# Other rates for the background work of VectorE in the first blocks of an RWKV and feed-forward layer, and three small transposes

## Chip, cores and metric

One core of one Trainium2 chip runs the whole layer. The metric is the device time of one execution in microseconds; of several executions the median counts. All data are 32-bit floats.

## What is computed

Input x has 2048 tokens of 512 channels. The reference, cut to what matters:

```python
def attn(x):                                  # x: tokens x 512
    h = layer_norm(x, ln1_g, ln1_b)
    hh = time_shift(h)                        # the token before, zero for the first
    k = (h * tm_mk + hh * (1 - tm_mk)) @ Wk.T
    v = (h * tm_mv + hh * (1 - tm_mv)) @ Wv.T
    r = (h * tm_mr + hh * (1 - tm_mr)) @ Wr.T
    x = x + sigmoid(r) * wkv(k, v, tm_first) @ Wo.T
    h = layer_norm(x, ln2_g, ln2_b)
    hh = time_shift(h)
    kk = (h * cm_mk + hh * (1 - cm_mk)) @ Wkey.T        # 2048 wide
    sr = sigmoid((h * cm_mr + hh * (1 - cm_mr)) @ Wcr.T)
    return x + sr * (silu(kk) @ Wval.T)

def ffn(h):
    gate, up = split(h @ w_gate_up.T, 2)                # 2 x 2048 wide
    return (silu(gate) * up) @ w_down.T

x = x + attn(layernorm(x))
x = x + ffn(layernorm(x))
```

Here wkv has an empty state: each token stands alone, so no recurrence runs along the tokens.

## The kernel before

**Blocks.** The tokens are cut into four blocks of 512. For each block b the kernel runs "units" on TensorE: k, r and v (time mix), out (Wo), gate (Wcr), four up units (Wkey), one down unit (Wval), and then for all blocks the feed-forward part. The order at the start is: k, r, v, out of block 0; k, r, v of block 1; gate of block 0; out of block 1; the up units and the down unit of block 0; then block 2 (lines 1335 to 1394).

**Products with fewer multiplications.** Most units (unit, line 541) multiply 2 x 2 blocks of matrices with seven products in place of eight. For that, sums of quarters of the weights are needed. prepare (line 147) makes them: GpSimd's queue loads the four raw quarters of a weight, VectorE makes four sums of 128 x 512, and GpSimd's queue stores each to memory. When a product needs a sum, weight (line 171) loads it over SyncE's queue into a ring of 12 buffers. The first units are plain (PLAIN, line 37; plain_unit, line 636): they use raw quarters and eight products. One product of eight records takes TensorE 1.73 us.

**Normalisation.** time_norm (line 757) treats one block: four moment steps on VectorE (bn_stats, bn_aggr), then affine (two small operations, var), then for block 1 the power -0.5 on GpSimd (line 413), four steps that scale 128 x 512 each into h (scaled, line 428), two pauses, then the transposes of h on TensorE, one chunk of four per step (transposed, line 440), with ScalarE taking each chunk out into hT. channel_norm (line 987) does the same for the second normalisation, and mix (line 488) blends hT with its shifted copy into the operand of a unit, with one blend on VectorE per chunk ("mix<-hT,vec,mix") and, for units that are not plain, four sums of the operand. residual (line 739) makes four steps of one small VectorE operation (shift) and one ScalarE operation.

first_block (line 824) handles block 0 without the planner. Its normed(j) makes moments, affine and the power on GpSimd (tile "two", line 842) for half of the block, and scales two 128 x 512 pieces into h. mixed(j) transposes them, and ScalarE and VectorE make the first operand of k. Ahead of that, TensorE runs 24 transposes of the identity matrix into the tile "warm" (lines 343 to 345) and 16 small products into accv and accx.

**The planner.** TensorE, VectorE and ScalarE run in the order in which the program writes instructions (manual_schedule, line 1331). Work beside the units stands in queues of generators: background (norms, mixes, residuals) and preps (the weight sums). After each product a unit calls tick (line 297), which decides how many background steps are written before the next product. Every VectorE operation adds its estimated time to spent (cost, line 208: 0.683 for a tensor operation over 512 elements, 0.535 for a scaling, 0.17 at least). The heart of tick is

```python
slack[0] = max(min(slack[0] + share[0] * length - spent[0], 2.5), -2.5)
credit[0] = min(credit[0] + credit[1], 2.0)
while slack[0] > 0 and (hot or background or preps):
    if preps and not hot and credit[0] >= 1 and prep_one():
        credit[0] -= 1
```

and otherwise one background step, with its cost taken off slack. So share is the part of TensorE's time that VectorE's background work may fill, and credit[1] is the number of weight sums per tick at most. A step that returns a value ("yield 1") is a pause: nothing more of that item in this turn, though another item may step; if none does, the tick ends. need (line 322) writes out whatever is left of an item when a unit requires it, and sets a positive slack to zero. need_sums (line 283) does so for weight sums. Operations put off with later (line 211) are written one or two products later and charged then.

share starts at SHARE0 = 0.95 and becomes SHARE = 0.88 after the first up unit of block 0 (line 1372). credit[1] is 0.7 from the first block's k unit on (line 1338), 0.67 after the first up unit of block 0 (line 1374), and 0.55 after the first up unit of block 1 (line 1376). Between two products the planner counts STEP = 1.72 us.

Of the kernel before, what the change touches and what calls it, by code (L numbers as in the profile page):

```python
# [9 lines left out]
F32 = mybir.dt.float32  # L10
# [5 lines left out]
P = 128  # L16
# [4 lines left out]
HB = TB // 2  # L21
# [1 line left out]
WAIT = 5  # L23
STEP = 1.72
SHARE = 0.88
SHARE0 = 0.95
WARM = 24
PP0 = -1e38

# [33 lines left out]
def rwkv_ffn_kernel(  # L63
# [9 lines left out]
    nc = tc.nc  # L73
# [11 lines left out]
    ps = ctx.enter_context(tc.tile_pool(name="ps", bufs=6, space=bass.MemoryType.PSUM))  # L85
# [16 lines left out]
    def tok_tile(name):  # L102
        return tokp.tile([P, NT, H], F32, tag="tok", name=name)

    def bank():
        return ps.tile([P, 2, HB], F32, tag="ps", name="ps")
# [82 lines left out]
    def load_x(b, queues=None):  # L189
        t = tok_tile("x")  # L190
        for k in range(NT):
            eng = queues[k] if queues else nc.sync
            paced(eng.dma_start(t[:, k, :], x_t[b][:, k, :]))
        return t
# [7 lines left out]
    slack = [0.0]  # L202
    share = [SHARE0]
    put_off = deque()
# [46 lines left out]
    credit = [0.0, 0.0]  # L251
# [64 lines left out]
    def push(name, gen, ready=None):  # L316
        background.append([ready, gen, name, False, background])
# [18 lines left out]
    ident = const.tile([P, P], F32, name="ident")  # L336
    make_identity(nc, ident)

    warm = const.tile([P, 1], F32, name="warm")
    nc.vector.memset(warm, 0.0)  # L340
    nc.scalar.activation(warm, warm, AF.Exp)

    pt = ps.tile([P, 2, HB], F32, tag="ps", name="warm")
    for _ in range(WARM):
        nc.tensor.transpose(pt[:, 0, 0:P], ident, ident)

# [17 lines left out]
    def constants():  # L364
        nc.vector.tensor_scalar(onem, vec[:, MK : CR + 1, :], -1.0, 1.0, ALU.mult, ALU.add)
        nc.vector.tensor_scalar(nfirst, vec[:, FIRST, :], -1.0, PP0, ALU.mult, ALU.add)
# [9 lines left out]
    def vcol(row, c):  # L376
        return vec[:, row, c : c + 1]
# [14 lines left out]
    def ts(out, *args):  # L392
        nc.vector.tensor_scalar(out, *args)  # L393
        cost(size(out), 0.1, 0.00085)

    def stt(out, *args):
        nc.vector.scalar_tensor_tensor(out, *args)  # L397
        cost(size(out))

    def moments(src, mv):  # L400
        for t in range(src.shape[1]):
            st = small.tile([P, 6], F32, tag="st", name="st")
            nc.vector.bn_stats(st, src[:, t, :])
            nc.vector.bn_aggr(mv[:, t, :], st)
            cost(512)
            cost(0)
            yield
# [71 lines left out]
    def op_tile(name):  # L479
        assert op_free(), name  # L480
        live_ops[0] += 1
        m = opp.tile([P, 7, 2, HB], F32, tag="op", name=name)
        return m, {"sums": set(), **{k: m[:, k] for k in range(7)}}
# [255 lines left out]
    def residual(b, xb, cols):  # L739

        x1 = tok_tile("x1")
        x1s[b] = x1
        for t, (mean, scale) in enumerate(cols):
            shift = small.tile([P, 1], F32, tag="shift", name="shift")
            stt(shift, mean, -1.0, scale, ALU.mult, ALU.mult)
            nc.scalar.activation(x1[:, t, :], xb[:, t, :], AF.Identity, bias=shift, scale=scale)
            spent[0] += 0.4
            yield

    def affine(var, mv):  # L750


        n = mv.shape[1]
        ts(var[:, :n], mv[:, :, 1], EPS, None, ALU.add)
        ts(var[:, n : 2 * n], mv[:, :, 1], 1.0 + EPS, EPS * EPS, ALU.mult, ALU.add)
# [68 lines left out]
    def first_block():  # L824


        xb = xin.pop(0)
        hT = htp.tile([P, NC, TB + 1], F32, tag="hT", name="hT_a")
        hTs[0, "a"] = hT
        h = tok_tile("h")  # L830
        m, B = op_tile("mix")
        ops[0, "k"] = B
        finished.add((0, "k"))
        cols = []

        def normed(j):
            mv = small.tile([P, 2, 2], F32, tag="mv", name="mv")
            yield from moments(xb[:, 2 * j : 2 * j + 2, :], mv)
            var = small.tile([P, 4], F32, tag="var2", name="var2")
            affine(var, mv)  # L840
            two = small.tile([P, 4], F32, tag="two", name="two")
            nc.gpsimd.tensor_tensor(two, var, mhalf[:, :4], ALU.pow)
            yield
            for t in range(2):
                cols.append((mv[:, t, 0:1], two[:, t : t + 1]))
                ts(
                    h[:, 2 * j + t, :],
                    xb[:, 2 * j + t, :],
                    mv[:, t, 0:1],
                    two[:, 2 + t : 3 + t],  # L850
                    ALU.subtract,
                    ALU.mult,
                )
                yield

        def mixed(j, other):
            at = slice(j * HB, (j + 1) * HB)
            by_one = slice(j * HB + 1, (j + 1) * HB + 1)
            for c in range(NC):
                pt = bank()  # L860
                for t in range(2):
                    nc.tensor.transpose(
                        pt[:, 0, t * P : (t + 1) * P],
                        h[:, 2 * j + t, c * P : (c + 1) * P],
                        ident,
                    )
                nc.scalar.activation(
                    hT[:, c, by_one],
                    pt[:, 0, :],
                    AF.Identity,  # L870
                    bias=vcol(LN1B, c),
                    scale=vcol(LN1G, c),
                )
                d = m[:, 2 * (c // 2) + j, c % 2, :]
                nc.scalar.activation(d, hT[:, c, at], AF.Copy, scale=onem[:, 0, c : c + 1])
                stt(d, hT[:, c, by_one], vcol(MK, c), d, ALU.mult, ALU.add)
                next(other, None)

        one, two = normed(0), normed(1)
        for _ in range(3):  # L880
            next(one)
        next(two)
        for _ in one:
            pass
        constants()
        nc.vector.tensor_copy(hT[:, :, 0:1], carry["a"])
        next(two)
        next(two)
        mixed(0, two)
        for _ in two:  # L890
            pass

        def second():
            mixed(1, iter(()))
            tails[0] = residual(0, xb, cols)
            nc.vector.tensor_copy(carry["a"], hT[:, :, TB : TB + 1])
            finished.add("norm0")
            slack[0] = spent[0] = 0.0

        return second  # L900
# [9 lines left out]
    def time_mix(b, name):  # L910
        row, n = {"k": (MK, WK), "r": (MR, WR), "v": (MV, WV)}[name]
        yield from mix((b, name), hTs[b, "a"], row, (b, n) in PLAIN)

    def push_mix(b, name, gen):
        norm = f"normb{b}" if name in ("cr", "ck") else f"norm{b}"

        alone = (0, "r") if (b, name) == (0, "v") else norm
        push((b, name, "t"), gen, lambda: {norm, alone} <= finished and op_free())
# [131 lines left out]
    def load_resid(b):  # L1050
        r = tok_tile("resid")
        paced(nc.sync.dma_start(r, resid[b]))
        loads[b] = r, load_x(b)
# [281 lines left out]
    second_half = first_block()  # L1335
    for n in "rv":
        push_mix(0, n, time_mix(0, n))
    credit[1] = 0.7
    k_unit(0)
    prepare_all(early, False, 2)  # L1340
    prepare_all([WVAL + 3] + [WK] + late, True, 1)
# [15 lines left out]
    for b in range(NB):  # L1357
        nxt = b + 2 < NB
        if nxt:
            xin[b + 2] = load_x(b + 2)  # L1360
        if b == NB - 1:
            load_resid(0)
        gate_unit(b)
        if b + 1 < NB:
            out_unit(b + 1)
        need((b, "ck"))
        if nxt:
            push(f"norm{b + 2}", time_norm(b + 2))
        for g in range(4):
            up_unit(b, g)  # L1370
            if b == 0:
                share[0] = SHARE
                if g == 0:
                    credit[1] = 0.67
            if b == 1 and g == 0:
                credit[1] = 0.55
            if g == 0:
                if nxt:
                    push_mix(b + 2, "k", time_mix(b + 2, "k"))
                    push_residual(b + 2)  # L1380
                    push_mix(b + 2, "r", time_mix(b + 2, "r"))
                if b + 1 < NB:
                    push(f"normb{b + 1}", channel_norm(b + 1))
                if nxt:
                    push_mix(b + 2, "v", time_mix(b + 2, "v"))
                if b + 1 < NB:
                    push_mix(b + 1, "cr", channel_mix(b + 1, "cr"))
                    push_mix(b + 1, "ck", channel_mix(b + 1, "ck"))
        if b == NB - 1:
            push((0, "z", "t"), ffn_in(0), op_free)  # L1390
        down_unit(b)
        if nxt:
            for n, u in (("k", k_unit), ("r", r_unit), ("v", v_unit)):
                u(b + 2)
# [95 lines left out]
```

## Time and profile before

| | us |
|---|---|
| three runs | 1239.83, 1241.60, 1241.62 |
| median | 1241.6 |
| the profiled execution, its own time | 1239.16 |
| its span from the first to the last instruction | 1237.4 |

| engine | busy us | share of the span | instructions |
|---|---|---|---|
| TensorE matmul | 1226.9 | 99% | 6516 |
| TensorE weight load | 1100.8 | 89% | 6516 |
| VectorE | 715.9 | 58% | 1321 |
| ScalarE | 359.4 | 29% | 666 |
| GpSimd | 155.1 | 13% | 278 |

In the profile PE is TensorE, PEld its weight load, DVE VectorE, ACT ScalarE, POOL GpSimd, SP SyncE; a q behind the name (SPq, POOLq) stands for its queue of DMA issues. L389 is line 389, out<-in names the tiles. A timeline row gives the start and the duration in microseconds, what ran and how often, and in brackets how long the engine had been idle before it and what it waited for. A row of the table of waits gives the total, the number and the longest of the waits of one kind.

VectorE's load is uneven. In a count by 40 slices of 31 us it is busy for 80% and more of the second to fourth slice (31 to 124 us) and of the sixth, while its mean is 58%.

### The profile page before, as it was taken

What the parts mean: (1) busy time and instruction counts of PE and PEld (TensorE: products, weight loads), DVE (VectorE), ACT (ScalarE), POOL (GpSimd) and SP (SyncE); (2) the same over time, 40 slices, a digit from 0 to 9 for tenths busy, and PEclk for the clock granted to TensorE, in tenths of its full rate; (3) what the DMA queues carried; (4) which work ended last, traced back from release to release, by engine and by line L of the source; (5) the groups of instructions that cost most, each with busy time, mean ns of one, the idle gap of its engine ahead of it and who ended that gap; (6) DMA issues with size and microseconds to landing.
All of it is one profiled execution on the core that took longest, in us unless ns stands there. A gap on an engine that the chain in (4) does not pass through costs nothing.

```text
span 1237.4 us, 18097 instructions
## 1 busy us (share of the span) xinstructions
PE 1226.9 (99%) x6516; PEld 1100.8 (89%) x6516; DVE 715.9 (58%) x1321; ACT 359.4 (29%) x666; POOL 155.1 (13%) x278
## 2 busy tenths in 40 slices
PE   9999999999999999999999999999999999999998
PEld 8888888888888888888888888998899888998898
DVE  5888587677675757532432365556546365462466
ACT  5534242242523425212311222212221222112211
POOL 2332322222212122221000000000000000000000
PEclk9999999999999999999999999999999999999999
DMA  5789997798887887897546655895469745785576
GB/s 195 257 273 300 312 346 265 251 335 296 286 258 244 294 273 241 257 322 261 153 142 193 216 144 156 267 338 152 145 186 306 270 142 152 244 292 160 151 215 213
DMA packets 140303, 294.06 MB, mean 238 GB/s; under 512 B 17576, under 2 KB 18744, under 8 KB 138936
## 3 DMA queue, kind: packets, MB, share of 16 engines
q1 hardware_dynamic: 117168, 219.99, 57.1%
q0 software_dynamic: 21440, 70.27, 15.9%
q10 hardware_dynamic: 1608, 2.65, 0.6%
q8 instruction: 53, 0.87, 0.3%
q14 instruction: 34, 0.28, 0.1%
HBM read 250.89 MB, written 41.95 MB: 237 GB/s over the span
## 4 chain that ended last, share of the span: by engine, by line
PE 93%; DMA 2%; DVE 1%; issue 1%; POOL 1%; ACT 1%; SPq 0%; DVEq 0%; ACTq 0%; POOLq 0%
PE ps L560 53%; PE ps L1214 14%; PE accv L560 10%; PE accx L560 10%; PE ps L662 4%; PE ps L445 1%; DMA w<-sum 1%; DMA raw<-in_w 1%; DMA row<-stats 1%; POOL q L152 0%; DMA x<-in_x 0%; DVE h L393 0%; ACT mix L498 0%; DVE resid L389 0%; DVE r L389 0%
## 5 line engine op out<-in xcount | busy, mean ns | idle before, releaser
L560 PE MATMUL ps<-zT,w 128*128 128x256 f32 x1280 | 289.5, 379 | 0.0
L560 PEld LDWEIGHTS ps<-zT,w 128*128 128x128 f32 x1280 | 241.9, 190 | 32.2
L560 PE MATMUL ps<-mix,w 128*128 128x256 f32 x960 | 220.0, 379 | 0.9 <-ACT u L591 0.9
L560 PEld LDWEIGHTS ps<-mix,w 128*128 128x128 f32 x960 | 181.9, 190 | 26.2 <-ACT u L591 1.7
L389 DVE TENSOR_TENSOR u<-u,accx 128x512 f32<-128x512 f32 x67 | 46.0, 686 | 137.1 <-ACT accx L595 137.1
L1214 PE MATMUL ps<-w,hid 128*128 128x128 f32 x832 | 104.5, 275 | 0.0
L560 PE MATMUL ps<-w,t 128*128 128x256 f32 x456 | 102.0, 379 | 0.0
L1214 PEld LDWEIGHTS ps<-w,hid 128*128 128x128 f32 x832 | 99.8, 192 | 0.8
L560 PEld LDWEIGHTS ps<-w,t 128*128 128x128 f32 x456 | 86.6, 190 | 11.7
L580 ACT COPY accv<-ps 128x512 f32<-128x512 f32 x67 | 38.2, 570 | 180.4 <-PE ps L560 177.6
L1214 PE MATMUL ps<-w,quads 128*128 128x128 f32 x704 | 89.0, 275 | 0.4 <-ACT r L1226 0.4
L1214 PEld LDWEIGHTS ps<-w,quads 128*128 128x128 f32 x704 | 84.2, 192 | 0.9 <-ACT r L1226 0.5
L595 ACT COPY accx<-ps 128x512 f32<-128x512 f32 x67 | 38.2, 571 | 159.5 <-PE ps L560 159.4
L389 DVE TENSOR_TENSOR u<-ps,u 128x512 f32<-128x512 f32 x67 | 46.3, 691 | 63.3 <-PE ps L560 63.2
L1308 POOL DMA_DIRECT2D out<-resid x12 | 8.6, 718 | 535.0 <-DVE resid L389 535.0
L591 ACT COPY u<-ps 128x512 f32<-128x512 f32 x67 | 39.2, 585 | 120.8 <-PE ps L560 120.8
L1226 ACT COPY r<-ps 128x128 f32<-128x128 f32 x112 | 29.8, 266 | 142.1 <-PE ps L1214 142.1
L389 DVE TENSOR_TENSOR raw<-raw 128x512 f32<-128x512 f32 x84 | 57.8, 688 | 12.3 <-issue 5.0
L560 PE MATMUL accv<-zT,w 128*128 128x256 f32 x256 | 60.6, 379 | 0.0
L560 PE MATMUL accx<-zT,w 128*128 128x256 f32 x256 | 60.5, 379 | 0.0
L560 PE MATMUL ps<-w,s 128*128 128x256 f32 x256 | 58.2, 379 | 0.0
L662 PE MATMUL ps<-mix,w 128*128 128x256 f32 x256 | 56.8, 380 | 1.1 <-DVE mix L397 1.1
(168 smaller groups left out, 1664.0 us busy)
## 6 DMA issues: line engine op xcount, KB each, us to landing
w<-sum SPq DMA_DIRECT2D x316, 256.0 KB, 3.4
w<-in_w SPq DMA_DIRECT2D x253, 256.0 KB, 3.4
w<-dd SPq DMA_DIRECT2D x112, 256.0 KB, 3.6
w<-d SPq DMA_DIRECT2D x48, 256.0 KB, 3.3
q<-in_w POOLq DMA_DIRECT2D x44, 256.0 KB, 6.2
sum<-q POOLq DMA_DIRECT2D x44, 256.0 KB, 4.6
raw<-in_w POOLq DMA_DIRECT2D x40, 256.0 KB, 5.8
sum<-raw POOLq DMA_DIRECT2D x40, 256.0 KB, 4.1
```

The costliest lines, as they stand in the source:

```text
L389: nc.vector.tensor_tensor(out, a, b, op)
L445: nc.tensor.transpose(flat[:, t * P : (t + 1) * P], h[:, t, c * P : (c + 1) * P], ident)
L560: mm = nc.tensor.matmul(pz[:, m, :], lhsT=lhsT, rhs=rhs, start=first and g == 0 and m == 0 and k == 0, stop=g == last and k == 1, skip_gro ...
L580: "z", A11, B11, True, pop_held, read=lambda: nc.scalar.copy(accv, acc["z"])
L591: nc.scalar.copy(tmp["u2"], acc["z"])
L595: nc.scalar.copy(accx, acc["z"])
L662: mm = nc.tensor.matmul(acc[i, j][:, m, :], lhsT=act[:, k, lo] if by_token else wg[:, k, lo], rhs=wg[:, k, :] if by_token else act[:, k, : ...
L1214: mm = nc.tensor.matmul(dst, lhsT=x[k][:, g, :], rhs=wt[:, g, :], start=first and g == 0, stop=g == 3, skip_group_check=True,)
L1226: nc.scalar.copy(st["r"][:, m, n * P : (n + 1) * P], st["z"])
L1308: eng.dma_start(out_t[b][:, tokens, cols], rs[b][:, tokens, cols])
```

## The change

It sets share to 1.0 from the start, until the last up unit of block 0 is written (it was 0.95, until the first up unit). It sets credit[1] to 0.64 up to the first up unit of block 0 (it was 0.7), and to 0.75 from there to the first up unit of block 1 (it was 0.67). In first_block it adds, after the power of the first half, three transposes of that power's result ("two", 128 x 4) into the tile "warm", which nothing reads.

```diff
-SHARE0 = 0.95
+SHARE0 = 1.0
...
-    pt = ps.tile([P, 2, HB], F32, tag="ps", name="warm")
+    pt = wt = ps.tile([P, 2, HB], F32, tag="ps", name="warm")
...
             nc.gpsimd.tensor_tensor(two, var, mhalf[:, :4], ALU.pow)
+            if j == 0:
+
+                for _ in range(3):
+                    nc.tensor.transpose(wt[:4, 0, 0:P], two, ident)
             yield
...
-    credit[1] = 0.7
+    credit[1] = 0.64
     k_unit(0)
...
             up_unit(b, g)
-            if b == 0:
+            if b == 0 and g == 0:
+                credit[1] = 0.75
+            if b == 0 and g == 3:
                 share[0] = SHARE
-                if g == 0:
-                    credit[1] = 0.67
             if b == 1 and g == 0:
                 credit[1] = 0.55
```

## The prediction

> **What bounds the kernel now.** I read the page first: its busy row, then the table of waits of TensorE, then the timelines of TensorE, VectorE, GpSimd and SyncE around each of those waits.
>
> ```profile
> span 1237.4 us, 18097 instructions
> PE 1226.9 (99%) x6516; PEld 1100.8 (89%) x6516; DVE 715.9 (58%) x1321; ACT 359.4 (29%) x666; POOL 155.1 (13%) x278
> ```
>
> TensorE sets the end. The change leaves its products as they are, so time can only come from its idle places or go into new ones. The table of its waits:
>
> ```profile
> PE ps L560 <- issue: 2.1, 1, 2.1
> PE warm L345 <- POOL ident masks.py:199: 1.4, 1, 1.4
> PE ps L662 <- DVE mix L397: 1.1, 1, 1.1
> PE ps L560 <- ACT u L591: 0.9, 2, 0.7
> PE ps L445 <- DVE h L393: 0.7, 1, 0.7
> ```
>
> Between the first product and the tail there are 2.1 + 0.9 + 0.7 = 3.7 us. That is the most the retuned rates can win, 0.3% of the time. The 2.1 us stand at 105 us, where the gate unit of block 0 starts (columns: start, duration, what; idle before in brackets):
>
> ```profile
> 105.03 0.69 DVE L389 TENSOR_TENSOR u<-ps,u 128x512 f32<-128x512 f32 x1 [0.38 <-PE ps L560]
> 105.64 0.68 DVE L389 TENSOR_TENSOR q<-q 128x512 f32<-128x512 f32 x1
> 106.24 2.73 DVE L397 SCALAR_TENSOR_TENSOR mix<-hT_b,vec,mix 128x512 f32<-128x512 f32 x4
> 107.08 2.18 PE L560 MATMUL ps<-w,mix 128*128 128x256 f32 x8 [2.09 <-issue]
> ```
>
> The label says "issue", but the order tells the cause. The four blends of the "cr" mix are put into VectorE's queue only when need((0, "cr")) forces them, behind the last addition of r_unit(1) and a weight sum (q<-q). The first blend ends near 106.95 and TensorE starts at 107.08.
>
> The 0.7 us stand at 44.6 us, where the transposes of block 1's h wait for VectorE:
>
> ```profile
> 38.31 0.24 DVE L393 TENSOR_SCALAR var<-mv 128x4 f32<-128x4 f32 x2
> 40.84 1.00 DVE L393 TENSOR_SCALAR h<-x,mv,two 128x512 f32<-128x512 f32 x2 [0.23 <-POOL two L413]
> 44.02 0.54 DVE L393 TENSOR_SCALAR h<-x,mv,two 128x512 f32<-128x512 f32 x1
> 43.28 0.60 PE L445 MATMUL ps<-ident,h 128*128 128x128 f32 x3
> 44.62 0.77 PE L445 MATMUL ps<-ident,h 128*128 128x128 f32 x5 [0.73 <-DVE h L393]
> ```
>
> VectorE has var at 38.55, GpSimd's root takes until 40.81, the fourth h starts at 44.02, and the transpose that reads it at 44.62.
>
> **Part 1, share 1.0 and credit 0.64 up to the first up unit.** Both are inputs of tick (lines 297 to 314): slack grows by share x 1.72 per tick, less what is charged, and while it is positive one step is put out, first a weight sum if credit is at least 1. So an exact order follows from the code. The charges are 0.683 for a 512-wide tensor op or sum, 0.853 for a moment step, 0.535 for an h, 0.57 for a residual step (0.17 + 0.4), 0.34 for affine, 0.17 + 0.4 for the first transposed chunk. r_unit(0) has eight ticks, r1 to r8. Slack starts at 0 (need resets it), and put-off additions charge 0.683 before r1, r2, r3, r5, r7. Four moment steps fill r1 to r3 in both kernels. From there, with slack after the tick:
>
> ```
>       before (0.95, 0.7)               after (1.0, 0.64)
> r3    -0.56                            -0.30
> r4    affine, 2 residual   -0.40       same                   -0.06
> r5    sum                  -0.14       sum, sum               -0.39
> r6    sum, h0, h1          -0.25       h0, h1, h2             -0.27
> r7    sum, h2              -0.52       sum, h3                -0.46
> r8    sum, h3              -0.11       2 residual, chunk 0    -0.45
> ```
>
> In r8 the new credit is 0.92 (0.64 after r6, 1.28 - 1 after r7, + 0.64), so no sum takes the slack of -0.46 + 1.72 = 1.26, and 1.26 - 0.57 - 0.57 still leaves 0.12 (time_norm's two pauses of lines 775 and 776 are each passed with a residual step in the same tick): chunk 0 of the transposes goes out at the end of r_unit(0). Before, chunk 0 came two ticks later, at 43.28. TensorE is in program order, so v_unit(0)'s products now stand behind those four transposes, and the whole TensorE queue behind them.
>
> When are they fed? The r unit ends at 17.04 + 104 x 0.2187 = 39.8 us (120 records run from 17.04 to 43.28; 104 of them are k and r). The work of VectorE up to var is the same, and it has no idle place from 27.1 us on, so the root still ends at 40.81. Then h0, h1, h2 at 0.46 each (40.84, 41.30, 41.76), the put-off e at 42.22, a sum at 42.82 (0.60 each by their starts), h3 at 43.42, and the fourth transpose 0.60 later by the row of before, at 44.02. TensorE has done 39.8 + 3 x 0.11 = 40.1 us of work by then: 3.9 us idle instead of 0.73, **a loss of 3.2 us**. Bounds: h0 to h3 back to back end at 42.7, a loss of 1.9; another 0.6 us op ahead, 3.8.
>
> For the gate unit I carry the same ledger on. Per tick the planner has 0.086 more to give out, and sums take 0.06 x 0.683 = 0.04 less. Over the 35 ticks up to there that is 4.4 us of its own time. channel_norm(0) gets its first moments 5 ticks earlier (before at 83.35), its transposes come 4 ticks earlier in one tick, and the first two blends of "cr" are put out 5 ticks ahead of the gate unit, the last two 3 ahead. One would do, so the wait goes: **a gain of 2.1 us**; at least 0.6, if only the one sum leaves the way. Four chunks of transposes in one tick need h3 of channel_norm(0), put out three ticks (5.2 us) before: by my chain of VectorE (moments, 1.4 us of root, four h) some 2.3 us early, no new wait. VectorE keeps up at share 1.0: an op charged 0.683 takes 0.60, so 1.72 charged is 1.51 us of a 1.73 us tick.
>
> **Part 2, credit 0.75 and share 1.0 through the up units.** From 107 us to the tail TensorE's only waits are the 0.65 and 0.22 us on ScalarE's u copy, behind a row load which the ledger leaves in its tick, so nothing is won. What is at risk is a sum that comes late. Sums of the four key units fall up to 4 ticks behind, with 7 or 8 ticks left to the load, and the ledger is level again at the last value group. The tight place is SyncE's queue:
>
> ```profile
> SPq L168 <- DMA sum<-raw: 13.4, 2, 9.2
> 179.50 13.37 SPq L168 DMA_DIRECT2D w<-sum  x4
> ```
>
> The fourth of these loads waits 9.2 us for the third sum of the last value group and holds all loads behind it until 192.9. It lands 3.4 us later; TensorE reads it at 198.46 + 3 x 1.73 = 203.6, so 7.3 us are in hand. In the new ledger that sum is one tick (1.7 us) later. Cost 0; without that cover it would be 1.7. Later sums come earlier, to nobody's gain.
>
> **Part 3, three root transposes.** They sit on TensorE ahead of the transposes of block 0's first h, which lead ScalarE, VectorE and the first product with no slack:
>
> ```profile
> 1.37 5.38 PE L345 MATMUL warm<-ident 128*128 128x128 f32 x24 [1.37 <-POOL ident masks.py:199]
> 7.89 1.06 PE L351 MATMUL accx<-ident 128*128 128x128 f32 x8
> 8.78 1.04 PE L862 MATMUL ps<-ident,h 128*128 128x128 f32 x8
> 6.41 1.04 POOL L842 TENSOR_TENSOR two<-var,mhalf 128x4 f32<-128x4 f32 x1 [5.10 <-DVE var L393]
> ```
>
> The root is there at 7.45, TensorE comes at 8.78, h is there: no wait, but 3 x 0.11 to 0.13 us: **+0.35 us**. Bounds: 0.2 with a shorter weight load, 0.65 at the slow rate of the first row (5.38 / 24 = 0.22).
>
> **Sum.** 0.35 + 3.2 - 2.1 = +1.45 us on the profiled execution: span 1237.4, with 1.76 around it 1239.16, so 1240.6. That execution lies 2.4 us under the median of the runs (1241.6; lowest 1239.83). I put the difference on the median: **1243.0**; own range +0 to +3.8, so 1241.6 to 1245.4.
>
> **Rivals.** (a) TensorE's rate falls after the long idle place: the likeliest slower case. The first row above is at 0.22 us per transpose, the third at 0.13 or less, though the granted clock reads 1.00 in both, so the trace has a slow state (transposes per half microsecond go from 4 to 7 at 7.5 us). Against: after 2.09 us of idle the product at 107.08 took 2.18 instead of 1.89, of which some 0.3 is its second blend, and no slow rate followed. For: no idle place of before is as long as 4.2 us with four transposes in it. If it decides, half the rate for at most as long as at the start (1.4 to 7.4) costs up to 3.0: 1243.0 to 1246.0, say 1245.3.
>
> [...]
>
> (b) The transposes of block 1 don't wait longer, because VectorE reaches var earlier than I think; the gate wait goes. Then -2.1 - 0.7 + 0.35 = -2.5: 1239.1. For: VectorE has 0.99 us idle at 26; against: the order of charges up to var doesn't change, and GpSimd's 2.17 us root lies between. (c) A sum comes over 7.3 us late, SyncE's queue runs dry: +1.45 + 3 = 1246; against it the single tick of delay. (d) That the change does nothing to the order would leave +0.35; the ledger excludes it.
>
> **Numbers.** Forecast 59%, (a) 28%, (b) 9%, (c) 4%. 0.2% (2.5 us) is about what a measurement can tell from no change. Faster: 7 of (b)'s 9. Slower: (a) but for 1, (c), and 12 of the forecast's upper end: 43. The rest, 50, lies within. The range runs from 1240.2 (a forecast that falls on a low run, as the profile did) to 1246.1 (the end of (a)).
>
> **What would show it.** L445 with some 4 us before it near 40 to 44 us, and v_unit(0)'s first product after it (step 1); no wait at the gate unit (part 1's gain); L662's first product near 11.2 instead of 10.88 (part 3); products at twice 0.22 us a record after 44 us would be (a). I am wrong if the first chunk of block 1 is not ahead of v_unit(0).

## The result, and the profile after

| | before | after |
|---|---|---|
| runs side by side on one chip | 11 | 11 |
| median us | 1240.86 | 1244.06 |
| lowest and highest | 1238.88, 1241.62 | 1243.19, 1244.88 |
| ratio of the times, with its 95% interval | | 1.0027 (1.0018 to 1.0037) |
| profiled execution: time, span | 1239.16, 1237.4 | 1244.06, 1242.0 |

The changed kernel is slower by some 3.3 us (0.0027 x 1240.86; 2.2 to 4.6 by the interval). The forecast was 1243.0, which is 1.45 us above the median of the three runs of before, and the range held the time. The case forecast, with no change of the clock, wasn't what happened: rival (a), the slower rate of TensorE after its long wait, came on top of it, and so did waits that the prediction had put at nothing. The profiled execution of before lies 1.7 us under the median of its eleven runs and that of the changed kernel on its median, so the two traces differ by more (4.9 us in time, 4.6 in span) than the medians do (3.2). The page of the changed kernel:

```profile
span 1242.0 us, 18100 instructions
PE 1229.2 (99%) x6519; PEld 1101.8 (89%) x6519; DVE 714.8 (58%) x1321; ACT 358.9 (29%) x666; POOL 154.7 (12%) x278
```

There are three more TensorE instructions (the root transposes), as many VectorE and ScalarE instructions as before, and a span that is 4.6 us longer. TensorE is busy 2.3 us longer, which three small transposes can't account for: the same products took longer. The table of TensorE's waits:

```profile
PE ps L445 <- DVE h L393: 3.1, 2, 1.8
PE ps L560 <- ACT u L591: 1.4, 2, 1.1
PE warm L345 <- POOL ident masks.py:199: 1.4, 1, 1.4
PE ps L560 <- ACT accx L595: 1.1, 2, 0.9
PE ps L662 <- DVE mix L397: 1.1, 1, 1.1
PE ps L1218 <- ACT r L1230: 0.4, 1, 0.4
```

The "issue" line of 2.1 us is gone. The wait for h has grown from 0.7 to 3.1 us in two parts, the waits for ScalarE's copies u from 0.9 to 1.4, and a line for its copies accx is new. No wait for a load of a weight appears. The timeline of TensorE around these places:

```profile
37.79 1.89 PE L662 MATMUL ps<-mix,w 128*128 128x256 f32 x8
41.47 1.24 PE L445 MATMUL ps<-ident,h 128*128 128x128 f32 x3 [1.79 <-DVE h L393]
44.04 0.33 PE L445 MATMUL ps<-ident,h 128*128 128x128 f32 x1 [1.33 <-DVE h L393]
44.21 5.31 PE L662 MATMUL ps<-mix,w 128*128 128x256 f32 x16
49.35 1.47 PE L445 MATMUL ps<-ident,h 128*128 128x128 f32 x12
...
109.93 1.89 PE L560 MATMUL ps<-w,mix 128*128 128x256 f32 x8
...
165.40 1.89 PE L560 MATMUL accx<-mix,w 128*128 128x256 f32 x8
168.38 5.45 PE L560 MATMUL ps<-mix,w 128*128 128x256 f32 x24 [1.09 <-ACT u L591]
174.72 1.99 PE L560 MATMUL ps<-mix,w 128*128 128x256 f32 x8 [0.89 <-ACT accx L595]
```

The four transposes of the first chunk stand ahead of v_unit(0), as the ledger gave it; behind them come two of its products (16 records), then the other twelve transposes. The row of 1.24 us for three transposes has idle time in it that the brackets don't show, since each waits for its own h: a transpose takes some 0.11 (the twelve at 49.35 start 0.11 apart). The fourth starts at 44.04. The gate unit starts at 109.93 with no wait. The row at 44.21 is the one to look at: 16 records in 5.31 us, while another row of 16 records (106.47, of the r unit) takes 3.62. The table by stretches of 1 us shows why (columns: stretch, its length, TensorE's busy time and records, granted clock, share of the DMA engines, GB/s):

```profile
43.00:44.00 1.00, 0.00 (x0) 1.00 0.65 246
44.00:45.00 1.00, 0.96 (x4) 0.71 0.09 37
45.00:46.00 1.00, 1.00 (x4) 0.50 0.60 225
46.00:47.00 1.00, 1.00 (x4) 0.50 0.32 98
47.00:48.00 1.00, 1.00 (x4) 0.59 0.43 164
48.00:49.00 1.00, 1.00 (x7) 1.00 0.04 8
```

Four records per microsecond while the granted clock is 0.50, seven just after it: the starts of the products' records lie 0.43 us apart before 47.8 us and 0.22 apart from there on. The half rate lasts 0.58 + 1 + 1 + 0.82 = 3.4 us (0.71 over a microsecond is 0.58 of it at half rate, 0.59 is 0.82), so it costs 1.7 us. VectorE's timeline of the same place:

```profile
38.34 0.24 DVE L393 TENSOR_SCALAR var<-mv 128x4 f32<-128x4 f32 x2
...
39.23 1.41 DVE L389 TENSOR_TENSOR q<-q 128x512 f32<-128x512 f32 x2
40.87 1.46 DVE L393 TENSOR_SCALAR h<-x,mv,two 128x512 f32<-128x512 f32 x3 [0.23 <-POOL two L413]
42.25 0.68 DVE L397 SCALAR_TENSOR_TENSOR e<-sg,e 128x512 f32<-128x512 f32 x1
42.85 0.68 DVE L389 TENSOR_TENSOR q<-q 128x512 f32<-128x512 f32 x1
43.45 0.54 DVE L393 TENSOR_SCALAR h<-x,mv,two 128x512 f32<-128x512 f32 x1
```

The prediction had these starts at 40.84, 42.22, 42.82 and 43.42 and the fourth transpose at 44.02; all came within 0.03 us. Between var and the h lies GpSimd's root, which took 2.17 us in both traces.

Where the span's 4.6 us come from, by comparing the start of each TensorE record with its predecessor's in both traces:

| place | forecast us | measured us |
|---|---|---|
| start, up to the first product | +0.35 | 0 |
| r unit of block 0 no longer waits for its mix (28.5 us) | 0 | -0.2 |
| transposes of block 1's h | +3.2 | +3.3 (4.2 idle, less 0.95) |
| half clock behind them | 0 (rival (a)) | +1.7 |
| gate unit of block 0 | -2.1 | -2.25 |
| a copy accx in a unit of block 1's time mix (99 us) | 0 | +0.4 |
| copies u and accx in the up and down units (167 to 341 us) | 0 | +1.9 |
| sum | +1.45 | +4.8 |

The sum is 0.2 over the measured difference, which is what such reading of single records leaves.

### The profile page after: what moved, and what is told of

It is laid out like the page before. It is cut to its first block, busy times and chain, and to the rows that moved or that the text cites. A ratio compares the mean times of both kernels' runs of the same rounds, so it can differ in the third digit from the quotient of the medians.

```text
span 1242.0 us, 18100 instructions
## 1 busy us (share of the span) xinstructions
PE 1229.2 (99%) x6519; PEld 1101.8 (89%) x6519; DVE 714.8 (58%) x1321; ACT 358.9 (29%) x666; POOL 154.7 (12%) x278
## 4 chain that ended last, share of the span: by engine, by line
PE 93%; DMA 2%; DVE 2%; issue 1%; ACT 1%; POOL 1%; SPq 0%; DVEq 0%; POOLq 0%; ACTq 0%
PE ps L560 52%; PE ps L1218 14%; PE accv L560 11%; PE accx L560 10%; PE ps L662 5%; PE ps L445 1%; DMA row<-stats 1%; DMA w<-sum 1%; DMA raw<-in_w 1%; DVE xT L389 1%; PE warm L345 0%; POOL q L152 0%; DVE t L389 0%; DVE q L389 0%; DVE resid L389 0%
```

## The experiments

Every kernel below ran in turn with the kernel before on the same chip, some 11 times; the ratio is to that kernel, with its 95% interval. "Before with" means the kernel before with only this edit.

**The root transposes alone.** Before with the third part of the change:

```diff
+            if j == 0:
+                for _ in range(3):
+                    nc.tensor.transpose(wt[:4, 0, 0:P], two, ident)
```

> The kernel before, with only the three root transposes added. Theory: they lie in TensorE's order ahead of the first transposes of h and cost 3 x 0.11 = 0.33 us wherever the slow state of the start ends, so the time rises by 0.3 us (0.2 to 0.65), and the first product of k starts 0.33 us later relative to the end of the 16 small products. Rival: they do something for TensorE's rate at the start or after the 1.06 us wait, and the time falls by 0.5 us or more.

Measured: 1240.24 against 1239.55, ratio 1.0001 (0.9993 to 1.001), that is -0.9 to +1.2 us. The three transposes take 0.33 us of TensorE in the trace, as priced. But the eight records into accv that come ahead took 1.05 us here, 1.21 in the changed kernel and 1.51 before, and the first product started at 10.71 here and at 10.91 there (10.88 before). In these three traces the first product starts between 10.71 and 10.91, and the one without the transposes lies between the two with them, so +0.35 and nothing can't be told apart; a gain of 0.5 us or more isn't seen in the median, though the interval doesn't exclude it. Nothing here shows that this part adds to the result.

**The front rates alone, and the late rates alone.** Before with share 1.0 and credit 0.64 up to the first up unit, and before with share 1.0 and credit 0.75 from there on:

```diff
-SHARE0 = 0.95
+SHARE0 = 1.0
...
-    credit[1] = 0.7
+    credit[1] = 0.64
```

> The kernel before, with only share 1.0 and credit 0.64 up to the first up unit (0.88 and 0.67 after it, as before). Theory: chunk 0 of block 1's transposes stands ahead of v_unit(0), TensorE idles about 4 us around 40 to 44 us (3 us more than before), the granted clock falls to 0.5 for one stretch of 3.4 us after it (1.7 us), the gate unit no longer waits (-2.25): +2.5 us in all, from +2 to +4. Rival: the loss of the full change comes from its other parts (the higher credit in the up units), and this kernel is not slower than before (-2 to 0).

```diff
-            if b == 0:
+            if b == 0 and g == 0:
+                share[0] = 1.0
+                credit[1] = 0.75
+            if b == 0 and g == 3:
                 share[0] = SHARE
-                if g == 0:
-                    credit[1] = 0.67
```

> The kernel before, with only share 1.0 and credit 0.75 from the first up unit on (share 0.88 again after the fourth). Up to there its order is that of before: waits of 0.73 us at 44 and 2.1 us at 105 us. Theory: ScalarE's steps of block 2's norm come a tick earlier than VectorE can feed them, ScalarE's copies queue behind them and TensorE waits some 1 us more near 165 to 175 us: +0.5 to +1.5 us. Rival: the waits there come only from the shifted start, and the time is that of before within 0.3 us.

Measured, front: 1242.7 against 1239.55, ratio 1.0023 (1.0014 to 1.0032), +2.8 us. The waits for h (1.79 and 1.33 in the brackets) and the half clock (0.83 as the mean of 40 to 50 us) are there, and the gate unit's wait is gone. All eleven executions have a mean granted clock of 0.997 or 0.998; of the 33 of before beside them, 19 have 0.999 or 1.000. Measured, late: 1243.09, ratio 1.0021 (1.0013 to 1.003), +2.6 us, with the order up to the first up unit as before. That is more than expected, and it contradicts the prediction's "cost 0" for part 2. In its table of TensorE's waits two lines are new, of which the second is short (0.3 us on accx), and one has grown; the first and the last of these:

```profile
PE accv L560 <- ACT sr L1008: 1.6, 1, 1.6
PE ps L560 <- ACT u L591: 1.5, 1, 1.5
```

The first of them, in the timelines of VectorE and TensorE:

```profile
282.30 1.42 DVE L389 TENSOR_TENSOR raw<-raw 128x512 f32<-128x512 f32 x2 [2.81 <-issue]
...
284.96 0.69 DVE L389 TENSOR_TENSOR e<-u,e 128x512 f32<-128x512 f32 x1
```

```profile
285.75 1.97 PE L560 MATMUL accv<-w,e 128*128 128x256 f32 x8 [1.55 <-ACT sr L1008]
```

The sums of raw quarters (raw<-raw) were put out sooner than VectorE could begin them: it stood for 2.81 us, and the additions behind them in program order, e<-u,e among them, came late by that and by the sums. The table puts TensorE's wait down to sr, but sr was done at 284.84 and e at 285.65, 0.1 us before the product that reads it; e is what it waited for. In the kernel before that e was done at 281.57, 4.1 us earlier, while the products around it were only 0.6 us earlier:

```profile
280.88 0.69 DVE L389 TENSOR_TENSOR e<-u,e 128x512 f32<-128x512 f32 x1
```

For VectorE's stand the timeline names no releaser ("issue"), but the view of the loads of the four raw quarters (line 152) does:

```profile
L152 POOL DMA_DIRECT2D raw<-in_w x4: 546/552/553, 270.7 to 273.2; - x4
  DVE raw L389: 2.8, 1
DMA to landing us min/median/max: 7.4/8.2/9.0
```

The last of them was issued at 273.2 and took 9.0 us to land, so it was there at 282.2, and VectorE began at 282.30: it stood because the quarters had not landed.

The two sums, +2.8 and +2.6, don't add up to the changed kernel's +3.3: it has no wait at 284 us. Why the front rates spare it that one was not followed up.

**Which of the two late rates it is.** Before with one of them each:

```diff
-                    credit[1] = 0.67
+                    credit[1] = 0.75
```

> The kernel before with only the credit raised from 0.67 to 0.75 from the first up unit of block 0 to that of block 1. Theory: the loss of the higher rates in the up units (+2.6 us with both) is the credit's: sums are put out sooner after their loads, VectorE stands in its order before a quarter that has not landed, and the additions and ScalarE's copies behind it come late (one wait of 1.5 us near 284 us): +1.5 to +2.6 us here. Rival: it is the share's, and this kernel is within 0.7 us of before.

```diff
-            if b == 0:
+            if b == 0 and g == 0:
+                share[0] = 1.0
+                credit[1] = 0.67
+            if b == 0 and g == 3:
                 share[0] = SHARE
-                if g == 0:
-                    credit[1] = 0.67
```

> The kernel before with only share 1.0 instead of 0.88 from the first up unit to the end of the fourth. Theory: ScalarE's norm steps come at most a tick earlier: 0 to +0.7 us. Rival: this is what costs +2.6 us in the kernel with both.

Measured, credit: 1242.79 (1240.03 to 1245.71) against 1240.21, ratio 1.0022 (1.0008 to 1.0036), with the same wait, at 284 us (0.7 us by the table of waits). Share: 1240.26, ratio 1.0002 (0.9991 to 1.0014). So by the medians the credit alone makes about the loss of both, and the share none that can be measured. How much of the credit's loss is waits is open: its profiled execution, a low one at 1240.72, has a span only 1.1 us over that of before, and its times go with the mean granted clock (the five executions at 0.999 or 1.000 have a median of 1240.25, the six at 0.996 to 0.998 one of 1243.9). Share did show something else, in TensorE's timeline and in the stretches of its profiled execution, the first two around the gate unit's wait and three around the wait for u:

```profile
166.64 5.62 PE L560 MATMUL ps<-mix,w 128*128 128x256 f32 x17 [1.92 <-ACT u L591]
```

```profile
103.01:106.42 3.41, 1.98 (x10) 1.00 1.00 366
106.42:109.83 3.41, 2.75 (x12) 1.00 0.87 247
...
164.45:167.86 3.41, 1.50 (x8) 1.00 0.68 247
167.86:171.27 3.41, 3.41 (x10) 0.50 0.61 198
171.27:174.68 3.41, 3.41 (x17) 1.00 0.91 289
```

A wait of 1.92 us was enough for another 3.4 us at half clock, from 167.86 to 171.27, while the gate unit's wait of 2.09 us in the same execution was not.

**The clock without the wait taken away.** The changed kernel, with 15 products of the identity matrix (30 records, which nothing reads) ahead of the first chunk of block 1's transposes:

```diff
+            for _ in range(15 if b == 1 and c == 0 else 0):
+                nc.tensor.matmul(flat[:, 0:P], lhsT=ident, rhs=ident, start=True, stop=True, skip_group_check=True)
```

> The changed kernel with 15 products of the identity (30 records, about 3.3 us of TensorE) ahead of chunk 0 of block 1's transposes, into the same bank, which the transposes then overwrite. They fill most of the idle place without doing anything for the result. Theory (the slow rate comes from the idle place): the granted clock stays at 1.0 after 44 us and v_unit(0)'s first 16 records take 3.6 us instead of 5.3; although work is added, the kernel is 1.5 to 2 us faster than the changed one, so about +1.5 us against before. Rival (the slow rate has another cause, or the fill delays what follows): no gain or a loss against the changed kernel, +3.2 us or more against before.

Measured: 1241.25, ratio 1.0011 (1.0002 to 1.002), so 0.0016, about 2.0 us, below the changed kernel by the ratios, whose intervals just overlap, with more work on the engine that sets the end. The mean granted clock of its eleven executions is 0.999 or 1.000; in the changed kernel's eleven it is 0.996 to 0.999. Its timeline of TensorE:

```profile
39.20 3.51 PE L445 MATMUL ps<-ident 128*128 128x128 f32 x30
42.54 0.49 PE L449 MATMUL ps<-ident,h 128*128 128x128 f32 x3
43.73 0.33 PE L449 MATMUL ps<-ident,h 128*128 128x128 f32 x1 [0.69 <-DVE h L393]
43.89 3.62 PE L666 MATMUL ps<-mix,w 128*128 128x256 f32 x16
```

The fourth transpose starts at 43.73, which is 4.4 us after the last product of the r unit has ended, as in the changed kernel (39.36 to 43.73 here, 39.68 to 44.04 there), because h is no earlier, but the 16 records behind it take 3.62 us in place of 5.31: 1.69 us, the half clock's price. The granted clock is 1.00 from 43 to 49 us. This separates the two costs: the wait is one, and the half clock that follows is the other.

**The wait taken away.** The changed kernel with the transposes of block 1 held back by the planner until some ticks have passed (a count in tick, and a loop of pauses in time_norm behind the four steps that scale h), and then the same hold with the front rates alone (credit 0.67 and share 0.88 in the up units as before, no root transposes):

```diff
+    ticks = [0]
...
+        ticks[0] += 1
...
-        if b == 1:
+        until = ticks[0] + (2 if b == 1 else 0)
+        while ticks[0] < until:
             yield 1
         yield 1
```

> The changed kernel, with the transposes of block 1 held back until three ticks later (chunk 0 then stands behind v_unit(0)'s first six products' worth of order instead of ahead of them). Theory: both idle places at 40 to 44 us go, the granted clock stays at 1.0, the gate unit still has its operand in time; what is left of the change's loss are the waits on ScalarE between 98 and 341 us (about 2.3 us). Against before -0.9 us (-2 to +0.5), against the changed kernel about -4. Rival: holding block 1 back moves the loss on (the gate unit waits again, or block 1's k mix comes late), and at most 1.5 us are won against the changed kernel.

> The kernel before with share 1.0 and credit 0.64 up to the first up unit and the same hold of block 1's transposes; old rates (0.88, 0.67) after the first up unit, no root transposes. Theory: the gain of the front rates alone, without their price: -2.25 at the gate unit, -0.95 at 44 us, about +1 in small waits on ScalarE: -2 us against before (-3 to -1). Rival: the front rates cost elsewhere in their own right, and the time is that of before within 0.7 us.

Measured, the first: 1237.03 (1236.54 to 1238.07) against 1240.21, ratio 0.9976 (0.9968 to 0.9985). The second: 1236.3 (1235.94 to 1236.82), ratio 0.9971 (0.9962 to 0.9981), 3.6 us faster than the kernel before and the best of all. Its timeline of TensorE at block 1's transposes:

```profile
33.68 10.96 PE L664 MATMUL ps<-mix,w 128*128 128x256 f32 x50
44.48 1.91 PE L447 MATMUL ps<-ident,h 128*128 128x128 f32 x16
46.22 4.05 PE L664 MATMUL ps<-mix,w 128*128 128x256 f32 x18
```

v_unit(0)'s products now run through the time in which the root and the h are made, and all sixteen transposes pass in one go without a wait. Of TensorE's waits for ScalarE's copies u and accx, the first kernel keeps 1.3 and 0.9 us, the second 1.0 and 0.3.

So the front rates were worth having: the same share and credit that lose 2.8 us win 3.6 when the consumer is not written ahead of its operand. The late rates and the root transposes, on top, give back 0.0005, some 0.6 us, within the two intervals. The mean granted clock is 0.999 or 1.000 in all executions of both.

**Share without credit in the front.** Before with SHARE0 = 1.0 only, which by the ledger writes the first chunk one tick later than both together:

```diff
-SHARE0 = 0.95
+SHARE0 = 1.0
```

> The kernel before with only share 1.0 up to the first up unit; credit stays at 0.7. Theory: in r8 the credit is 1.1, a sum takes the slack, and chunk 0 comes one tick later, behind two more chunks of v: the idle place before the fourth transpose's h shrinks from 4 to about 2.4 us (part of it with transposes in between), the gate wait goes all the same: within 0.7 us of before where the clock holds, with 1.7 us more in executions where it doesn't. So the price is set by the tick in which chunk 0 falls. Rival: share 1.0 alone costs as much as both (+2.5 us or more), whatever the tick.

Measured: 1240.9 against 1239.8, ratio 1.0008 (0.9999 to 1.0016), +1.0 us where both knobs gave +2.8. Its timeline of TensorE:

```profile
41.20 1.24 PE L445 MATMUL ps<-ident,h 128*128 128x128 f32 x3
43.77 0.47 PE L445 MATMUL ps<-ident,h 128*128 128x128 f32 x1 [1.33 <-DVE h L393]
```

One product more stands ahead, so of the 4.2 us of idle time 2.5 are left (0.23 + 0.35 + 0.34 + 1.55 between the starts, beyond what a record takes). The clock still fell, for 3.4 us from about 43.8 on. So the idle place shrinks with the tick in which the first chunk falls, as the ledger would have it. The time can't be put down to it alone: the interval just includes no loss, and TensorE has two other waits in this trace that the kernel before doesn't have in this size, 1.9 us for a copy u at 167 us and 1.5 us for a copy accv at 323 us.

**The gate unit's wait filled.** Before with nine products of the identity matrix ahead of the gate unit of block 0 (fill is 9 there and 0 elsewhere), to see whether the 2.1 us wait of the kernel before brings half clock in some of its executions:

```diff
+                for _ in range(fill):
+                    nc.tensor.matmul(flat(acc[z])[:, 0:P], lhsT=ident, rhs=ident, start=True, stop=True, skip_group_check=True)
```

> The kernel before with nine products of the identity (18 records, 1.95 us of TensorE) ahead of the gate unit of block 0, into the bank that the unit then clears: they fill the 2.25 us wait there and compute nothing that is used. Theory: that wait, too, sends TensorE to half rate in some executions (before spreads from 1237.9 to 1244.3, the held kernels over 1.5 us); filled, it cannot, and the median falls by 0.3 to 1.5 us with fewer runs above 1241, though no work is taken away. Rival: the spread comes from the start or from elsewhere; the median is that of before within 0.2 us and so is the spread.

Measured: 1239.12 (1238.54 to 1240.73) against 1239.8 (1238.65 to 1243.49), ratio 0.9996 (0.9987 to 1.0004). The direction is as expected and no time is over 1241 us, but the interval includes no change, and three of the twelve executions still have a mean clock of 0.998 (11 of the 23 of before have 0.997 or 0.998): inconclusive.

What can be said of the kernel before goes by the mean granted clock of its 32 executions beside the second group of kernels:

| mean granted clock | executions | median us |
|---|---|---|
| 1.000 | 5 | 1238.0 |
| 0.999 | 10 | 1239.2 |
| 0.998 | 15 | 1240.9 |
| 0.997 | 2 | 1243.2 |

3.4 us at half clock take 0.5 x 3.4 / 1240 = 0.0014 off the mean and cost 1.7 us. A row is not a count of such stretches, though: the clock also falls behind the last product, where it costs nothing (in the profiled execution of before for the last 1.1 us, in that of the credit alone for 2.4, which is 0.0010 of the mean). An estimate from these figures is that 0.998 and less needs a stretch among the products. So much of the spread of the kernel before goes along with such stretches, but not all of what the clock's mean shows is time: the eleven executions of the changed kernel, at 0.996 to 0.999, lie within 1.7 us. The best kernel's ten executions lie within 0.9 us, those of before within 6.3. Which waits bring them in which execution of the kernel before is open.

## Why the prediction was right, and where it was short

**What bounds the kernel: right.** All of the time went into or came out of TensorE's idle places and its clock.

**Part 1, the transposes: right in mechanism and size.** The ledger's order came out as worked through; the loss of 3.2 us was 3.3. Its bounds (1.9 and 3.8) were not needed.

**Part 1, the gate unit: right.** -2.1 was -2.25, the whole of the wait.

**The clock: the step that failed.** The forecast took full rate after the idle time and gave the half rate to rival (a), at 28%, with up to 3.0 us. It struck in the profiled execution, cost 1.7 us, and was there in the trace of the front rates alone and of share alone too; filling the idle time took it away. The argument against it was that 2.09 us of idle time before the gate unit were followed by no slow rate. That row is no accident of one execution: the wait stands in five of the traces (before, the roots alone, and the three of the late rates), and behind it the granted clock is 1.00, to 115 us in the kernel before, in both late rates and in the credit alone, and to 109.83 in share alone in the up units. But it could not carry the weight, since the length of a wait isn't what decides: 1.92 us sufficed at another place of one of these traces, and the kernel before has a mean clock of 0.997 or 0.998 in 17 of 32 executions. The idle time was to be 3.9 us, and the rival should have had the larger chance.

The traces show what goes with it. The half clock lasts 3.41 us in share alone in the up units (167.86 to 171.27) and in the changed kernel (44.41 to 47.83; 3.413 by the record of the clock in that trace). That record has a second fall, at 1242.49, behind the last instruction: 1198.08 us after the first, which is 351.0 times 3.413 (1198.08 / 351 = 3.4133). With a trace divided into stretches of that length, counted from a fall, the stretch ahead of the fall has TensorE idle for 1.65 us in share alone in the front, 1.91 at 164.45 above, 2.06 in the changed kernel, and 2.83 in the kernel before, whose clock falls at 1236.27, behind the last product. In the last two traces the most in a stretch with no fall behind it is 1.47 us in the kernel before, at its gate unit, and 1.35 in the changed kernel (from 7.47 and 6.87 us on, where the records of the clock begin). So the 1.92 us lay within one stretch (busy 1.50 of 3.41), while the gate unit's 2.09 us were split over two (busy 1.98 and 2.75). Where the stretches begin differs from trace to trace: near the gate unit at 103.04 in the kernel before, at 102.44 in the changed one. This is a pattern of four traces; no kernel moves a wait from one stretch into two to test it.

**Part 2, "cost 0": failed.** The prediction looked for the risk in late loads of sums on SyncE's queue, and no wait of TensorE for such a load came up. The cost came from the other side, work written too early. Of the late rates alone, +2.6 us, the credit makes nearly all by the medians, and sums written before their quarters have landed hold VectorE up. In the changed kernel the +1.9 us of waits on ScalarE's copies between 167 and 341 us are mostly this step's: with the transposes cured, the held kernel keeps the larger two of them (1.2 and 1.05 us, by the starts of the records) with the late rates and has 0.7 and 0.45 without. How one of them arises can be followed in ScalarE's timeline, first of the kernel before, then of the changed one:

```profile
168.44 0.81 ACT L816 ACTIVATE hT_a<-xT,vec 128x512 f32<-128x512 f32 x1 [2.61 <-DVE xT L389]
169.16 0.58 ACT L595 COPY accx<-ps 128x512 f32<-128x512 f32 x1
169.77 0.81 ACT L816 ACTIVATE hT_a<-xT,vec 128x512 f32<-128x512 f32 x1
```

```profile
171.44 0.81 ACT L816 ACTIVATE hT_a<-xT,vec 128x512 f32<-128x512 f32 x1 [3.11 <-DVE xT L389]
...
173.37 0.81 ACT L816 ACTIVATE hT_a<-xT,vec 128x512 f32<-128x512 f32 x1 [0.63 <-DVE xT L389]
174.09 0.58 ACT L595 COPY accx<-ps 128x512 f32<-128x512 f32 x1
```

The same three instructions in another order. Before, the copy accx stood between two steps of the norm of block 2; with more given out per tick, the second of these was written a tick earlier, and the copy, for which TensorE has to wait at 174.72, stands behind it and with it behind VectorE's xT. The 0.4 us at 99 us is alike, in the front: the copy accx of 98.80 stands behind four steps hT_b that fill ScalarE from 96.14 on. The prediction followed the queues of VectorE and SyncE through the new ledger, but not ScalarE's.

**Part 3: not resolved.** +0.35 was 0 in the pair of traces, because the slow rate of the start ended earlier in one of them (the eight records into accv took 1.51 us before and 1.21 after; TensorE goes from 4 or 5 records per half microsecond to 7 at 7.5 us before and at 7.0 after), and anywhere from -0.9 to +1.2 us in the runs.

**The number.** 1243.0 was near 1244.06 partly by its base: it stood on the median of three runs, 1241.6, and eleven runs gave 1240.86. That is luck: the increase forecast, 1.45 us, was under half of the 3.3 measured. In the pair of traces the two missing terms are the clock's 1.7 and the 2.3 on ScalarE's copies; the medians differ by less than the traces, which fits the mean clock of the kernel before: many of its executions seem to have slow stretches too.

## What to carry to other kernels

Where an engine runs in program order, a background rate that is raised moves consumers as well as producers; hold each consumer until its operand is due (here behind GpSimd's root and four h), and the same rates turn from 2.8 us lost into 3.6 us won. When an idle place of TensorE is made longer, price the clock behind it with the wait (here 1.7 us more), and follow every in-order engine through the new order, ScalarE's short copies included. More background work per step wins nothing where it only brings an engine to a load that hasn't come in (2.81 us of VectorE up to 282 us).

## What was unexpected of the hardware

The granted clock fell to 0.50 for 3.4 us after idle times of TensorE of 1.92 us (share alone in the up units), 2.5 us in pieces (share alone in the front) and 4.2 us in pieces (the changed kernel), and didn't after 2.09 us ahead of the gate unit in four traces. What these three falls have in common is 1.65 us or more of idle time (1.91, 1.65 and 2.06) within the 3.41 us just ahead of them, which is as long as the half clock itself lasted. The four transposes within the 4.2 us didn't prevent it; 30 records of products with the identity did, and useless work on the engine that sets the end made the kernel 2.0 us faster.
